# Turning one pass's x and results in 32x32 squares on VectorE instead of with TensorE transposes

## The chip, the cores and the metric

The kernel runs on one core of a Trainium2 chip. The metric is the device time of one execution in microseconds (us); less is better. Five engines matter. TensorE (PE in the profile; PEld is its weight load) multiplies matrices and writes the result to PSUM banks. VectorE (DVE), ScalarE (ACT) and GpSimd (POOL) work element by element. SyncE (SP) issues the transfers between memory (HBM) and the on-chip SBUF. Each engine carries out its own instructions strictly in order, and waits for other engines through semaphores.

## The reference

A layer of nine experts (eight gated by a probability per image, one shared) is added to its input. x holds 8 images of 512 rows by 256 features; an expert has a hidden width of 1,024.

```
g = einsum('bsd,edf->ebsf', h, Wg)
u = einsum('bsd,edf->ebsf', h, Wu)
expert_outs = einsum('ebsf,efd->ebsd', silu(g) * u, Wd)
expert_output = einsum('be,ebsd->bsd', gating_probs, expert_outs)
shared = (silu(h @ Sg) * (h @ Su)) @ Sd
x + (1 - sg) * expert_output + sg * shared
```

All of it is float32. Nothing in a row s of an image depends on another row, so the rows may stand in any order while they are worked on, if the same order is undone at the end.

## The kernel before

**Passes and units.** The 8 images are worked on in two passes (`h` = 0 and 1) of four images. A pass goes over 9 experts and 2 halves of the hidden width, so there are 36 units in all; a unit takes 66.9 us in the steady part of the trace. A unit has the "up" part, `gate_up` (products with Wg and Wu), and the "down" part of the unit before it, `down` (products with Wd), woven together by hand.

**The tiling.** The products use an algebraic scheme for fewer multiplications: for each of four images (index `i`) and each of six pairs of images (`PAIRS`), sums and differences of x and of weights are multiplied. For a pair the kernel needs three forms of x: `v`, a scaled difference, and two sums `b`. x has to stand turned for this, features on partitions and the 512 rows s along the free axis, in two halves `k` of 128 features. In the first pass `turn_x` makes the turned x and the first unit makes the forms (lines 238 and 252) and stores them to a scratch area in HBM (`store_forms`). All later units of the pass load the forms from there (lines 242 and 259: `v` has three buffers, `b` two).

**The second pass's x.** During the first pass `prepare(1)` makes the second pass's forms ahead of time: load an image in rows, turn it with TensorE transposes against the identity into a PSUM bank (`turn`, line 145, four 128x128 transposes make one turn of 128 features by 512 rows), copy it to SBUF with ScalarE (line 194) or combine it with VectorE (line 196), store it to `xdram`, load it back pair by pair, make the forms with GpSimd (lines 213 to 219) and store them (line 224). It is a generator. The main loop takes one step of it at every fifth "down" step from the third unit on, so its TensorE and GpSimd instructions stand between those of the units.

**The first pass's results.** They add up in SBUF tiles, `accb` and `accB`, one for each image and half of the features, features on partitions. When the pass closes, `turn_back` brings them back into rows: a turn of four transposes into a bank, then one VectorE addition of x's rows (line 634), and a store to `out` (line 635). x's rows come from `load_back` (line 616). The eight blocks of the first pass are turned back inside the second pass's first unit, at the "down" steps in `BACK_AT`, in the order of `BACK`. The second pass's results are turned at the end by the `h + 1 == NH` branch of the same function.

**The order of the work.** TensorE's and GpSimd's instructions are in the order in which the program writes them (`manual_schedule`), ScalarE's as well in the first unit. The order on the other engines and queues is chosen by a planner from its own idea of durations. All loads and stores go through SyncE's one queue, and every transfer there also waits for the landing of the one issued eight before it. The two PSUM banks that the down part shares with the turns are handed out by `new_po`; `turned[n]` notes that a turn used the bank last.

**Buffers.** The pool `io`, four buffers of 2 KB per partition, holds the rows, the turned blocks and the forms of `prepare`, and the rows of `load_back`.

Of the kernel before, what the change touches and what calls it, by code (L numbers as in the profile page):

```python
# [16 lines left out]
def kernel(  # L17
# [68 lines left out]
    dpool = ctx.enter_context(tc.tile_pool(name="d", bufs=2))  # L86
    iopool = ctx.enter_context(tc.tile_pool(name="io", bufs=4))
    dram = ctx.enter_context(
# [58 lines left out]
    def load_rows(pool, tag, b):  # L147
        rows = []
        for c in range(2):
            t = pool.tile([P, 2, D], F32, tag=tag, name=f"xin{b}_{c}")  # L150
            nc.sync.dma_start(
                t, x[b].rearrange("(p t) d -> p t d", t=NT)[:, 2 * c : 2 * c + 2, :]
            )
            rows.append(t)
        return rows

    def turn_x(h, rows):

        for i in range(NI):
            xt = xpool.tile([P, 2, S], F32, tag="x", name=f"x{h}_{i}")  # L160
            for n_, k in enumerate((0, 1) if CI[i] == 0.0 else (1, 0)):
                pt, n = new_po(f"ptx{h}_{i}_{k}")
                turn(pt, [rows[i][t // 2][:, t % 2, ts(k, P)] for t in range(NT)])
                turned[n] = True
# [12 lines left out]
    def prepare(h):  # L177

        def tile_of(name):
            return iopool.tile([P, S], F32, tag="io", name=f"{name}{h}")  # L180

        for i in range(NI):
            to = xdram[h, i] = dram.tile([P, 2, S], F32, tag=f"xd{h}_{i}", name=f"xd{h}_{i}")
            rows = load_rows(iopool, "io", NI * h + i)
            yield
            yield
            both = {}
            for k in (1, 0):
                pt, n = new_po(f"ptx{h}_{i}_{k}", True)
                turned[n] = True  # L190
                turn(pt, [rows[t // 2][:, t % 2, ts(k, P)] for t in range(NT)])
                both[k] = tile_of(f"xt{i}_{k}_")
                if k == 1 or CI[i] == 0.0:
                    nc.scalar.copy(both[k], pt)
                else:
                    ve.scalar_tensor_tensor(both[0], both[1], -CI[i], pt, ALU.mult, ALU.add)  # L196
                yield
            yield
            for k in (1, 0):
                nc.sync.dma_start(to[:, k], both[k])  # L200
            yield
        for p, (i, j) in enumerate(PAIRS):
            d = CI[i] - CI[j]
            to = dram.tile([P, 3, S], F32, tag=f"xs{h}_{p}", name=f"xs{h}_{p}")
            at = []
            for n, k in ((i, 0), (j, 0), (j, 1), (i, 1)):
                t = tile_of(f"f{p}_{n}_{k}_")
                nc.sync.dma_start(t, xdram[h, n][:, k])
                at.append(t)
            yield  # L210
            yield
            v = at[0]
            gp.tensor_tensor(v, v, at[1], ALU.subtract)
            if d != 1.0:
                gp.tensor_scalar(v, v, 1.0 / d, 0.0, ALU.mult, ALU.add)
            yield
            gp.tensor_tensor(at[2], v, at[2], ALU.add)
            yield
            gp.tensor_tensor(at[3], v, at[3], ALU.add)
            yield  # L220
            yield
            yield
            for k, n in ((0, 0), (1, 2), (2, 3)):
                nc.sync.dma_start(to[:, k], at[n])
            scratch[h, p] = to
            yield
# [380 lines left out]

    BACK = [(0, 1), (0, 0), (1, 1), (2, 1), (1, 0), (2, 0), (3, 1), (3, 0)]

    def block_of(a, b, r):  # L610
        return a[b].rearrange("(p t) d -> p t d", t=NT)[:, :, ts(r, P)]

    def load_back(h, i, r, pool=None, tag="io"):
        if (h, i, r) not in back:
            xr = (pool or iopool).tile([P, NT, P], F32, tag=tag, name=f"xr{h}_{i}_{r}")
            nc.sync.dma_start(xr, block_of(x, NI * h + i, r))
            back[h, i, r] = xr
        return back[h, i, r]

    def turn_back(h, i, r):  # L620

        b = NI * h + i
        block = ends.pop((h, i, r))
        pt, n = new_po(f"pto{b}_{r}", h + 1 < NH)
        turned[n] = True
        turn(pt, [block[:, ts(t, P)] for t in range(NT)])
        pt = pt.rearrange("p (t d) -> p t d", t=NT)
        if h + 1 == NH:
            for c, xr in enumerate(last_rows[i]):
                part = xr[:, :, ts(r, P)]  # L630
                ve.tensor_add(part, pt[:, 2 * c : 2 * c + 2], part)
            return
        xr = load_back(h, i, r)
        ve.tensor_add(xr, pt, xr)
        nc.sync.dma_start(block_of(out, b, r), xr)
        n = BACK.index((i, r)) + 1
        if n < len(BACK):
            load_back(h, *BACK[n])

# [128 lines left out]
    since_close = 1000  # L768
    BACK_AT = (5, 7, 9, 11, 14, 17, 20, 23)
    HAND = {mybir.EngineType.PE, mybir.EngineType.Pool}  # L770
# [20 lines left out]
    for u in units:  # L791
# [6 lines left out]
        for what in FIRST if u.n == 0 else LAST if nxt is None else ORDER:  # L798
            if what == "G":
# [6 lines left out]
                if final and nxt is not None and nG in (18, 21, 24, 27):  # L806
                    load_x(u.h + 1, (nG - 18) // 3)
                if nxt is None and nG == 40:
                    for i in range(NI):
# [77 lines left out]
```

## Time and profile before

| What | Value |
|---|---|
| time, median of 3 runs | 2461.21 us (2460.86 to 2461.64) |
| the profiled execution | 2461.27 us, span 2459.3 us |
| granted TensorE clock | 0.999 |
| loads (all `xin`, both passes, 256 KB each) | 24 |
| rows loaded by `load_back` (`xr`, 256 KB each) | 8, 3.1 us from issue to landing |
| results stored from `xr` (256 KB each) | 8, 3.5 us from issue to landing |
| `v`, `b` loaded from the scratch area | 210 each, 2.6 and 3.6 us |

One execution is profiled. The page gives for every engine its busy time and share of the span, and splits the span into 40 slices. A group of instructions has one line: source line, engine, operation, what it writes and reads, count, busy time, mean duration of one in ns, and the idle time of its engine just before it with the engine that ended it. The chain of waits is followed back from the last instruction, at each step to what released it. A busy time of TensorE includes the overlap of a matmul with the next, so two records that start 0.43 us apart show 0.59 us each. A float32 product shows as two records.

### The profile page before, as it was taken

To read this page: it belongs to the slowest core of one execution; us is meant where nothing else is said; L and a number is where in the kernel's file an instruction comes from. 1 tells how busy PE (TensorE), PEld (TensorE's weight loads), DVE (VectorE), ACT (ScalarE), POOL (GpSimd) and SP (SyncE) were. 2 spreads that over 40 slices of the span, in tenths; PEclk is the share of its full clock that TensorE was granted. 3 is DMA by queue.
4 is the path that set the end of the run, shared out by engine and by line. 5 is a ranking of instruction groups with operands and counts; after the bars stand their busy time and mean duration, and the time that the engine had idled before them with its cause. 6 is when DMAs were issued, how large, how long until landed. Compare 5 with 4: busy or idle time off the path is not lost.

```text
span 2459.3 us, 22816 instructions
## 1 busy us (share of the span) xinstructions
PE 2440.4 (99%) x5782; PEld 1084.0 (44%) x5782; DVE 1931.9 (79%) x2876; ACT 1246.4 (51%) x2305; POOL 2092.8 (85%) x2335
## 2 busy tenths in 40 slices
PE   9999999999999999999999999999999999999998
PEld 4444444444444444444444444444444444444444
DVE  7777787787777777777987777778777777777787
ACT  4555445545555555455455555555555555555543
POOL 7988888898898998888878888888888888888883
PEclk9999999999999999999999999999999999999999
DMA  5333333443333333333443233223333333223332
GB/s 168 95 93 103 97 113 107 124 132 107 109 115 94 119 97 106 110 116 113 127 144 94 88 90 98 86 86 99 99 103 103 94 103 90 86 89 96 91 93 82
DMA packets 180801, 255.83 MB, mean 104 GB/s; under 512 B 14016, under 2 KB 114368, under 8 KB 180672
## 3 DMA queue, kind: packets, MB, share of 16 engines
q1 hardware_dynamic: 180384, 254.33, 34.1%
q8 instruction: 49, 0.80, 0.1%
q14 instruction: 80, 0.66, 0.1%
q10 hardware_dynamic: 288, 0.04, 0.0%
HBM read 238.59 MB, written 15.73 MB: 103 GB/s over the span
## 4 chain that ended last, share of the span: by engine, by line
PE 89%; POOL 6%; DVE 2%; issue 1%; ACT 0%; DMA 0%; DVEq 0%; POOLq 0%; ACTq 0%
PE c L461 28%; PE c L451 14%; PE c L429 9%; PE c L407 9%; PE r L547 7%; PE r L570 7%; PE S L531 5%; PE b L531 5%; PE q L547 5%; PE s L547 2%; POOL cols L488 2%; POOL rows L488 1%; POOL wb L345 0%; DVE h L398 0%; POOL wb L346 0%
## 5 line engine op out<-in xcount | busy, mean ns | idle before, releaser
L461 PE MATMUL c<-b,wb 128*128 128x512 f32 x1728 | 847.3, 592 | 0.0
L393 ACT ACTIVATE sg<-c 128x512 f32<-128x512 f32 x576 | 343.6, 597 | 590.0 <-DVE c L466 336.9
L398 DVE SCALAR_TENSOR_TENSOR h<-sg,coef,c 128x512 f32<-128x512 f32 x576 | 428.1, 743 | 247.5 <-PE c L461 139.8
L461 PEld LDWEIGHTS c<-b,wb 128*128 128x128 f32 x1728 | 327.8, 190 | 410.0 <-issue 388.7
L451 PE MATMUL c<-v,u 128*128 128x512 f32 x864 | 441.7, 593 | 0.4 <-ACT c L446 0.3
L488 POOL TENSOR_TENSOR rows<-rows,h 128x512 f32<-128x512 f32 x282 | 371.1, 1316 | 0.0
L456 DVE TENSOR_TENSOR c<-D,c 128x512 f32<-128x512 f32 x432 | 299.1, 693 | 78.5 <-ACT sg L393 58.5
L488 POOL TENSOR_TENSOR cols<-cols,h 128x512 f32<-128x512 f32 x282 | 359.9, 1276 | 0.0
L466 DVE TENSOR_TENSOR c<-c,D 128x512 f32<-128x512 f32 x432 | 298.8, 692 | 20.1 <-PE c L461 19.9
L345 POOL TENSOR_TENSOR wb<-u,wb 128x256 f32<-128x256 f32 x108 | 79.0, 732 | 237.3 <-ACT wb L343 237.3
L407 PE MATMUL c<-x,w 128*128 128x512 f32 x576 | 277.9, 595 | 0.3 <-DVE x L168 0.3
L451 PEld LDWEIGHTS c<-v,u 128*128 128x128 f32 x864 | 162.9, 190 | 205.9 <-issue 165.3
L547 PE MATMUL r<-h,wd 128*128 128x512 f32 x426 | 217.7, 592 | 0.2 <-DVE xt L196 0.2
L570 PE MATMUL r<-X,ud 128*128 128x512 f32 x426 | 217.6, 592 | 0.0
L477 DVE TENSOR_TENSOR X<-h,h 128x512 f32<-128x512 f32 x213 | 210.4, 988 | 6.9
L429 PE MATMUL c<-x,at 128*128 128x512 f32 x432 | 209.6, 593 | 2.5 <-DVE P L422 2.2
L439 ACT COPY D<-c 128x512 f32<-128x512 f32 x284 | 165.9, 584 | 87.2 <-DVE h L398 87.2
L488 POOL TENSOR_TENSOR rows<-h,h 128x512 f32<-128x512 f32 x144 | 198.4, 1378 | 0.0
L488 POOL TENSOR_TENSOR cols<-h,h 128x512 f32<-128x512 f32 x144 | 184.2, 1279 | 0.0
L412 ACT COPY P<-c 128x512 f32<-128x512 f32 x216 | 126.6, 586 | 111.4 <-PE c L407 107.0
L407 PEld LDWEIGHTS c<-x,w 128*128 128x128 f32 x576 | 109.1, 191 | 135.0 <-issue 112.1
L530 ACT COPY S<-accS 128x512 f32<-128x512 f32 x134 | 79.1, 590 | 150.4 <-DVE accV L518 142.6
(105 smaller groups left out, 3482.4 us busy)
## 6 DMA issues: line engine op xcount, KB each, us to landing
b<-xs SPq DMA_DIRECT2D x210, 512.0 KB, 3.6
v<-xs SPq DMA_DIRECT2D x210, 256.0 KB, 2.6
w<-in_L_cond_Wg_dram SPq DMA_DIRECT2D x128, 128.0 KB, 3.5
w<-in_L_cond_Wu_dram SPq DMA_DIRECT2D x128, 128.0 KB, 3.6
wd<-in_L_cond_Wd_dram SPq DMA_DIRECT2D x32, 512.0 KB, 4.9
xin<-in_x_dram SPq DMA_DIRECT2D x24, 256.0 KB, 3.4
f<-xd SPq DMA_DIRECT2D x24, 256.0 KB, 3.2
xs<-f SPq DMA_DIRECT2D x18, 256.0 KB, 2.0
```

The costliest lines, as they stand in the source:

```text
L393: nc.scalar.activation(s, bank, AF.Silu)
L398: ve.scalar_tensor_tensor(t, u.sg[i, j], coef[:, u.e, b : b + 1], bank, ALU.mult, ALU.mult)
L407: nc.tensor.matmul(bank, u.raw[i][:, m, 0], xhub[u.h, i][:, 0], start=True, stop=True)
L429: nc.tensor.matmul(bank, u.at[i][:, m], xhub[u.h, i][:, 1], start=False, stop=True, skip_group_check=True,)
L451: nc.tensor.matmul(bank, u.U[p][:, m], u.V[p], start=False, stop=True, skip_group_check=True)
L456: ve.tensor_sub(other, u.Ds[j, m], bank)
L461: nc.tensor.matmul(bank, u.W[p][:, r, m], u.VB[p][:, r], start=False, stop=True, skip_group_check=True,)
L466: ve.tensor_add(bank, bank, u.Ds[j, m])
L488: gp.tensor_tensor(sums[n], u.h_[n, n] if first else sums[n], u.h_[at], ALU.add)
L531: nc.tensor.matmul(po, w, b, start=not full, stop=True, skip_group_check=full)
L547: nc.tensor.matmul(po, w, b, start=True, stop=True)
L570: nc.tensor.matmul(A, u.Ud[p], u.X[p], start=False, stop=True, skip_group_check=True)
```

## The change

The second pass's x and the first pass's results are no longer turned by TensorE. VectorE's `transpose` takes a 128x512 tile as a grid of 32x32 squares and turns each square by itself, leaving the square where it is. The squares are brought to their places by the transfers:

- `load_turned` loads an image for `prepare` with eight DMAs in place of two. Each takes 32 features of the image to 32 partitions, in runs of 32 elements (128 bytes). Two VectorE transposes and one subtraction (none for image 0) give the turned x. The copies on ScalarE fall away.
- The first pass's rows s stand in another order along the free axis, such that a square of a result block holds 32 features of rows 16 apart: `turn_x` writes its transposes into the bank with a stride.
- `turn_back` transposes a result block in squares into a tile of the pool `z`, and adds it to x's rows, which `load_back` has loaded in squares (four DMAs per image, runs of 128 bytes). Both halves of an image share a tile, and are stored with four DMAs, in runs of 128 bytes. The end of the second pass is turned as before.
- `BACK`, `BACK_AT` and the places of the first loads differ: images 0 and 2 are loaded in the last unit of the first pass, image 1 takes the tile of image 0 after its store, image 3 that of image 2.
- The pool `io` has two buffers of 4 KB in place of four of 2 KB, and the forms of `prepare` load both halves of an image at once.

```diff
--- before.py
+++ after.py
@@ -84,7 +84,7 @@
     zpool = ctx.enter_context(tc.tile_pool(name="z", bufs=6))
     spool = ctx.enter_context(tc.tile_pool(name="s", bufs=4))
     dpool = ctx.enter_context(tc.tile_pool(name="d", bufs=2))
-    iopool = ctx.enter_context(tc.tile_pool(name="io", bufs=4))
+    iopool = ctx.enter_context(tc.tile_pool(name="io", bufs=2))
     dram = ctx.enter_context(
         tc.tile_pool(name="dram", bufs=1, space=bass.MemoryType.DRAM)
     )
@@ -147,20 +147,43 @@
     def load_rows(pool, tag, b):
         rows = []
         for c in range(2):
-            t = pool.tile([P, 2, D], F32, tag=tag, name=f"xin{b}_{c}")
+            if pool is not iopool:
+                t = pool.tile([P, 2, D], F32, tag=tag, name=f"xin{b}_{c}")
+            elif c == 0:
+                both = pool.tile([P, NT, D], F32, tag=tag, name=f"xin{b}")
+            if pool is iopool:
+                t = both[:, 2 * c : 2 * c + 2]
             nc.sync.dma_start(
                 t, x[b].rearrange("(p t) d -> p t d", t=NT)[:, 2 * c : 2 * c + 2, :]
             )
             rows.append(t)
         return rows
 
+
+    def squares(a, b, q):
+
+        return a[b].rearrange("s (k q d) -> q s k d", k=2, d=32)[q]
+
+    def load_turned(to, b):
+
+
+        at = x[b].rearrange("(c r t) d -> r t c d", r=32, t=NT)
+        for k in (1, 0):
+            for q in range(4):
+                nc.sync.dma_start(
+                    to[ts(q, 32), k].rearrange("r (t c d) -> r t c d", t=NT, d=32),
+                    at[:, :, :, ts(4 * k + q, 32)],
+                )
+
     def turn_x(h, rows):
 
         for i in range(NI):
             xt = xpool.tile([P, 2, S], F32, tag="x", name=f"x{h}_{i}")
             for n_, k in enumerate((0, 1) if CI[i] == 0.0 else (1, 0)):
                 pt, n = new_po(f"ptx{h}_{i}_{k}")
-                turn(pt, [rows[i][t // 2][:, t % 2, ts(k, P)] for t in range(NT)])
+                at = pt.rearrange("d (l t h) -> d t h l", l=4, h=32)
+                for t in range(NT):
+                    nc.tensor.transpose(at[:, t], rows[i][t // 2][:, t % 2, ts(k, P)], ident)
                 turned[n] = True
                 if k == 1:
                     nc.scalar.copy(xt[:, 1], pt)
@@ -177,51 +200,48 @@
     def prepare(h):
 
         def tile_of(name):
-            return iopool.tile([P, S], F32, tag="io", name=f"{name}{h}")
+            return iopool.tile([P, 2, S], F32, tag="io", name=f"{name}{h}")
 
         for i in range(NI):
             to = xdram[h, i] = dram.tile([P, 2, S], F32, tag=f"xd{h}_{i}", name=f"xd{h}_{i}")
-            rows = load_rows(iopool, "io", NI * h + i)
-            yield
-            yield
-            both = {}
+            rows = tile_of(f"xin{i}_")
+            load_turned(rows, NI * h + i)
+            yield
+            yield
+            both = tile_of(f"xt{i}_")
             for k in (1, 0):
-                pt, n = new_po(f"ptx{h}_{i}_{k}", True)
-                turned[n] = True
-                turn(pt, [rows[t // 2][:, t % 2, ts(k, P)] for t in range(NT)])
-                both[k] = tile_of(f"xt{i}_{k}_")
-                if k == 1 or CI[i] == 0.0:
-                    nc.scalar.copy(both[k], pt)
-                else:
-                    ve.scalar_tensor_tensor(both[0], both[1], -CI[i], pt, ALU.mult, ALU.add)
+                ve.transpose(both[:, k], rows[:, k])
+                if k == 0 and CI[i] != 0.0:
+                    ve.scalar_tensor_tensor(
+                        both[:, 0], both[:, 1], -CI[i], both[:, 0], ALU.mult, ALU.add
+                    )
                 yield
             yield
             for k in (1, 0):
-                nc.sync.dma_start(to[:, k], both[k])
+                nc.sync.dma_start(to[:, k], both[:, k])
             yield
         for p, (i, j) in enumerate(PAIRS):
             d = CI[i] - CI[j]
             to = dram.tile([P, 3, S], F32, tag=f"xs{h}_{p}", name=f"xs{h}_{p}")
-            at = []
-            for n, k in ((i, 0), (j, 0), (j, 1), (i, 1)):
-                t = tile_of(f"f{p}_{n}_{k}_")
-                nc.sync.dma_start(t, xdram[h, n][:, k])
-                at.append(t)
-            yield
-            yield
-            v = at[0]
-            gp.tensor_tensor(v, v, at[1], ALU.subtract)
+            at = {}
+            for n in (i, j):
+                at[n] = tile_of(f"f{p}_{n}_")
+                nc.sync.dma_start(at[n], xdram[h, n])
+            yield
+            yield
+            v, B_i, B_j = at[i][:, 0], at[i][:, 1], at[j][:, 1]
+            gp.tensor_tensor(v, v, at[j][:, 0], ALU.subtract)
             if d != 1.0:
                 gp.tensor_scalar(v, v, 1.0 / d, 0.0, ALU.mult, ALU.add)
             yield
-            gp.tensor_tensor(at[2], v, at[2], ALU.add)
-            yield
-            gp.tensor_tensor(at[3], v, at[3], ALU.add)
-            yield
-            yield
-            yield
-            for k, n in ((0, 0), (1, 2), (2, 3)):
-                nc.sync.dma_start(to[:, k], at[n])
+            gp.tensor_tensor(B_j, v, B_j, ALU.add)
+            yield
+            gp.tensor_tensor(B_i, v, B_i, ALU.add)
+            yield
+            yield
+            yield
+            for k, made in enumerate((v, B_j, B_i)):
+                nc.sync.dma_start(to[:, k], made)
             scratch[h, p] = to
             yield
 
@@ -605,37 +625,39 @@
                     ends[u.h, i, r] = acc["bB"[r], i]
             yield
 
-    BACK = [(0, 1), (0, 0), (1, 1), (2, 1), (1, 0), (2, 0), (3, 1), (3, 0)]
-
-    def block_of(a, b, r):
-        return a[b].rearrange("(p t) d -> p t d", t=NT)[:, :, ts(r, P)]
-
-    def load_back(h, i, r, pool=None, tag="io"):
-        if (h, i, r) not in back:
-            xr = (pool or iopool).tile([P, NT, P], F32, tag=tag, name=f"xr{h}_{i}_{r}")
-            nc.sync.dma_start(xr, block_of(x, NI * h + i, r))
-            back[h, i, r] = xr
-        return back[h, i, r]
+    BACK = [(0, 1), (0, 0), (2, 1), (2, 0), (1, 1), (1, 0), (3, 1), (3, 0)]
+
+    def load_back(h, i):
+
+        if (h, i) not in back:
+            xr = iopool.tile([P, S // 32, 2, 32], F32, tag="io", name=f"xr{h}_{i}")
+            for q in range(4):
+                nc.sync.dma_start(xr[ts(q, 32)], squares(x, NI * h + i, q))
+            back[h, i] = xr
+        return back[h, i]
 
     def turn_back(h, i, r):
 
         b = NI * h + i
         block = ends.pop((h, i, r))
-        pt, n = new_po(f"pto{b}_{r}", h + 1 < NH)
-        turned[n] = True
-        turn(pt, [block[:, ts(t, P)] for t in range(NT)])
-        pt = pt.rearrange("p (t d) -> p t d", t=NT)
         if h + 1 == NH:
+            pt, n = new_po(f"pto{b}_{r}")
+            turned[n] = True
+            turn(pt, [block[:, ts(t, P)] for t in range(NT)])
+            pt = pt.rearrange("p (t d) -> p t d", t=NT)
             for c, xr in enumerate(last_rows[i]):
                 part = xr[:, :, ts(r, P)]
                 ve.tensor_add(part, pt[:, 2 * c : 2 * c + 2], part)
             return
-        xr = load_back(h, i, r)
-        ve.tensor_add(xr, pt, xr)
-        nc.sync.dma_start(block_of(out, b, r), xr)
-        n = BACK.index((i, r)) + 1
-        if n < len(BACK):
-            load_back(h, *BACK[n])
+        xr = load_back(h, i)
+        t = zpool.tile([P, S], F32, tag="z", name=f"to{b}_{r}")
+        ve.transpose(t, block)
+        ve.tensor_add(xr[:, :, r], t.rearrange("p (c d) -> p c d", d=32), xr[:, :, r])
+        if (i, 1 - r) not in BACK[BACK.index((i, r)):]:
+            for q in range(4):
+                nc.sync.dma_start(squares(out, b, q), xr[ts(q, 32)])
+            if i in (0, 2):
+                load_back(h, i + 1)
 
     last_rows = {}
     tails = {}
@@ -766,7 +788,7 @@
 
     ends = {}
     since_close = 1000
-    BACK_AT = (5, 7, 9, 11, 14, 17, 20, 23)
+    BACK_AT = (5,10,11,13,15,18,20,23)
     HAND = {mybir.EngineType.PE, mybir.EngineType.Pool}
     by_hand = ExitStack()
     by_hand.enter_context(
@@ -805,6 +827,8 @@
                     behind = down(u, acc)
                 if final and nxt is not None and nG in (18, 21, 24, 27):
                     load_x(u.h + 1, (nG - 18) // 3)
+                if final and nxt is not None and nG in (30, 36):
+                    load_back(u.h, (nG - 30) // 3)
                 if nxt is None and nG == 40:
                     for i in range(NI):
                         last_rows[i] = load_rows(
```

## The prediction

> **What bounds the kernel now.** I read the page first, its engine row and its chain of waits; then the groups by form; then the chain around the change of passes, the busy time by stretches, and the DMA queues in short windows. From the page:
>
> ```profile
> PE 2440.4 (99%) x5782; PEld 1084.0 (44%) x5782; DVE 1931.9 (79%) x2876; ACT 1246.4 (51%) x2305; POOL 2092.8 (85%) x2335
> ```
>
> TensorE is busy for 99% of the span, and in the steady units the chain is TensorE alone. A product counts as two records of 0.43 us there, so what leaves TensorE shortens the run by its own length, unless another engine is the late one at that place. Two places are such: the first 100 us and some 15 us after the change of passes. The sum is made against the profiled execution, 2461.27 us; its span is 2459.3 us, and the median of the runs shown is 2461.21 us, 0.06 us lower, so no correction is needed.
>
> The groups by form (the first within 150 to 450 us; count, then busy us and mean ns, then idle time before and who ended it):
>
> ```profile
> L145 PE MATMUL ptx<-ident,xin 128*128 128x128 f32 x32 | 4.9, 276 | 1.8 <-ACT accS L539 1.8
> ...
> L477 DVE TENSOR_TENSOR X<-h,h 128x512 f32<-128x512 f32 x213 | 210.4, 988 | 6.9
> ...
> L168 DVE COPY x<-ptx 128x512 f32<-128x512 f32 x1 | 0.7, 691 | 5.7 <-PE ptx L145 5.7
> ```
>
> The chain after the change of passes (start, us, what):
>
> ```profile
> 1239.83 0.68 DVE xr L634
> 1240.51 1.20 DVE accb L522 x2
> 1241.71 1.41 DVE P L422 x3
> 1243.12 0.29 issue
> 1243.41 1.88 DVE P L422 x3
> 1245.29 0.61 DVE accB L518
> 1245.90 0.04 issue
> 1245.95 0.66 PE pto L145 x4
> 1246.60 0.86 PE c L451 x2
> ...
> 1257.34 0.44 PE pto L145 x4
> ```
>
> Here VectorE is the late engine from 1239.8 to 1245.9 us. From 1246 us on TensorE is again, and a turn of four transposes costs 0.44 us of chain.
>
> Busy time by stretches (us: length, then PE, PEld, DVE, ACT, POOL with their counts, clock, DMA share, GB/s):
>
> ```profile
> 12.00:48.00 36.00, 34.13 (x90) 14.55 (x88) 35.15 (x49) 19.21 (x39) 31.93 (x39) 1.00 0.46 160
> 48.00:66.00 18.00, 18.00 (x42) 7.50 (x42) 15.01 (x19) 9.10 (x19) 18.00 (x18) 1.00 0.41 136
> 1250.00:1283.00 33.00, 33.00 (x94) 15.54 (x93) 24.74 (x36) 17.49 (x33) 20.69 (x22) 1.00 0.64 192
> ```
>
> VectorE is full in the first stretch (35.15 of 36 us) and has room in the other two.
>
> **Part 1, the second pass's x.** Eight turns leave TensorE's order: 8 x 0.44 = 3.5 us. With them goes the 1.8 us in which TensorE stood ahead of them, waiting until ScalarE had emptied the shared bank (first group row). Behind them the ordinary products follow, whose inputs are ready; nothing else is late there. Gain 5.3 us. Five ScalarE copies of 0.59 us go too, hidden now and then.
>
> In their place come eight turns on VectorE and the three subtractions that were there before. Their order isn't written by hand, and in the changed program's order they have all moved to the first two units: two transposes stand between the forms of v at about 31 and 36 us, three instructions between 48 and 66 us, six between 78 and 103 us. No 32x32 turn is in this trace. The nearest row is the 128x512 float32 copy, 0.69 us. The Trainium skill, page "VectorE: DVE Perf Modes", section "The three transpose paths", gives 311 ns for 128x128 in bf16; four of those make 1.24 us, an estimate. It speaks against the change: 0.55 us more for each of 16 turns. I take the row, which has this size and type; 1.24 us is the upper end, and the 0.34 us of the fastest VectorE instruction on 128x512 here (v, L240 at 41.69 us: 0.41 us, with its overlap removed) the lower.
>
> The first two stand in a full stretch: 2 x 0.69 = +1.4 us, between 0.7 and 2.5. The next three are 2.1 us in a stretch with 3.0 us of VectorE idle. But TensorE takes nothing there that is ready long before, so between nothing and 2.1 us; I take the middle, +1.0. The last six fall where VectorE has 8.5 us idle of 32 (66 to 98 us) and more after: nothing, at most 1 us if they stand ahead of a wanted subtraction.
>
> SyncE's order gains 32 loads of 512 runs for eight of 128. A load of 512 runs held its queue for 0.55 us (xr, L616), so 17.6 us in place of about 3, all from 12 to 103 us, past the stores of v and b, the weights and the first v and b of unit 1. The queue stands idle for more than half of that time. The nearest need behind it is the third weight tile of unit 1, issued at 56.8 us, landing 3.6 us later and used by GpSimd at 67.7: 7 us of cover against four loads, 2.2 us. Two transposes, at about 51 and 62 us, may wait for their last load up to 1 us; that is in the bounds above. Stores of the turned x wait for VectorE with other transfers queued behind, but the turns stand well ahead of those transfers' own waits. Nothing more taken.
>
> The first pass's 32 transposes now write their bank in strides of 32 and 4 places. No strided write to a bank is in this trace: between nothing and a doubling of 8 x 0.44 us. I take nothing, for loads of x hold this stage.
>
> **Part 2, the pass's results.** Eight turns leave TensorE. The first two stand in the VectorE-bound stretch: there the first turn and addition on VectorE (0.69 + 0.99 for 0.68 us) make the chain 1.0 us longer, which eats the two turns of 0.44 and most of the 0.6 us of waiting for accB at 1245.3. I count these as zero. The six others give 6 x 0.44 = 2.6 us.
>
> VectorE pays. An addition no longer reads a bank but two operands beside GpSimd's work, like X: 0.99 us in place of 0.69. By the changed order, seven turns and seven additions fall between 1250 and 1283 us, where five additions stood: 24.74 - 5 x 0.69 + 7 x 0.69 + 7 x 0.99 = 33.1 us, in a stretch that TensorE would now do in 33 - 5 x 0.44 = 30.8 us. **VectorE becomes the bound there** by 2.3 us: loss 2.3, from nothing (additions at 0.69, the rest fitted around) to 5.
>
> **The transfers of part 2.** Rows of 512 bytes become squares of 128: per image 4,096 packets, 256 on each of 16 DMA engines. Two windows, 0 to 9 us and 1290 to 1294 us, give the price of a packet (packets, MB, share):
>
> ```profile
> q10 hardware_dynamic: 288, 0.04, 2.3%
> ```
> ```profile
> q1 hardware_dynamic: 672, 0.79, 64.6%
> ```
>
> The first is the gates, packets of 256 bytes and fewer: 2.3% of 16 x 9 us is 3.3 us, 11.5 ns a packet. The second is one store of 512-byte rows and 128 packets of 4 KB: 41.3 us, of which the large ones at 19 GB/s take 27.6, so about 27 ns per 512-byte row. For 128 bytes I take 11.5 ns, an image 2.9 us. The rule against it is in the Trainium skill, page "DMA: Bandwidth & Descriptors", "Specifications": under 512 bytes the DMA reads, modifies and writes. Nothing in this trace shows a short store. By the rule a store might cost two 512-byte accesses, 54 ns, 13.8 us an image.
>
> SyncE's queue: by four points (0.32 us at 128 runs, 0.55 at 512) 1,024 runs hold it about 0.86 us, an image 3.5 us. The order is: four stores of image 0 (ready about 1254 us), the b of the third pair, four loads of image 1, which wait for those stores, four stores of image 2, then the b of the fourth pair. That b went out here:
>
> ```profile
> 1265.64 0.38 SPq L259 DMA_DIRECT2D b<-xs  x1
> ```
>
> Its product starts at 1275.0 us, some 1274 without the turns. Now it lands at 1254 + 3.5 + 2 (stores landed) + 3.5 + 3.5 + 3.5 + up to 1 = about 1271: cover 3 us, no cost. With packets over 13.7 ns the packets rule in place of the issues: 1259.5 + 0.768 us per ns, which reaches 1274 at **19 ns**. Beyond that TensorE waits.
>
> **Sum:** 2461.27 - 5.3 + 1.4 + 1.0 - 2.6 + 2.3 = 2458.1; I say 2458.0 us.
>
> **Rivals.**
> A, **short packets (slower):** place, b of the fourth pair; from 19 ns. At 27 ns it lands at 1280.2: +6.2, 2464 us. With stores at 54 and loads at 27 it lands at 1294: +20, 2478 us; with loads at 11.5, +16, 2474. For it: the rule, and a DMA share of 0.64 already in that stretch. Against: the gates' packets, which are loads.
> B, **VectorE hides it:** startup and overload fit into idle time, only the turns count: 2461.27 - 5.3 - 3.5 = 2452.5 us. For it: VectorE's 79%; against: the full first stretch.
> C, **slow turn** (1.24 us): +0.55 for two turns at the start, about 1 for the next, 8 x 0.55 at the change of passes: +6.5, 2464.5 us. For it the skill's figure, against it the rows[...], all 0.69.
>
> **How the numbers follow.** Forecast 0.38, A 0.30, C 0.14, B 0.18. A measurement of this kernel tells about 0.2% (4.9 us) from no change: bounds 2456.3 and 2466.1. Faster: B and 0.12 of the forecast, 0.30. Slower: 0.26 of A (which may add to C) and 0.08 of C, 0.34. Within: 0.36. The range goes from B to A's stores at 54 ns with loads at 11.5: 2452 to 2474; the forecast's own is 2454 to 2462.
>
> **What would show it.** Right: no TensorE wait ahead of a turn at 180 to 430 us; TensorE some 2 us later at 100 us; VectorE near full from 1250 to 1283; the turn at 0.6 to 0.7 us; 128-byte packets near 12 ns, and no wait of b's products for a DMA. Wrong: b's products waiting for xs at 1265 to 1290, VectorE waiting for loads of x, or a turn over 1 us.

## The result, and the profile after

| | Kernel before | Kernel after |
|---|---|---|
| time, median | 2460.91 us (2460.62 to 2461.64) | 2454.39 us (2453.63 to 2455.2) |
| the profiled execution's span | 2459.3 us | 2452.9 us |
| granted TensorE clock | 0.999 | 0.999 |

The ratio is 0.9974, with a 95% interval of 0.9965 to 0.9983: the changed kernel is 6.5 us faster, between 4.2 and 8.6. That is 3.6 us below the forecast of 2458.0, at the lower end of its own range (2454 to 2462), and by 1.6 us past the 4.9 us that the forecast took for the limit of "no change"; it had given 0.30 to such a gain.

From the page of the kernel after, the engine row:

```profile
PE 2432.8 (99%) x5718; PEld 1077.7 (44%) x5718; DVE 1940.2 (79%) x2890; ACT 1245.8 (51%) x2304; POOL 2094.4 (85%) x2335
```

TensorE has 64 records less: sixteen turns of four. Its busy time fell by 7.6 us, VectorE's rose by 8.3.

Busy time by stretches, kernel after, the three stretches that the forecast used:

```profile
12.00:48.00 36.00, 33.36 (x90) 14.63 (x88) 34.48 (x50) 18.71 (x37) 30.58 (x38) 1.00 0.57 180
48.00:66.00 18.00, 16.94 (x40) 6.80 (x39) 15.50 (x20) 8.14 (x18) 16.64 (x16) 1.00 0.54 165
...
1250.00:1283.00 33.00, 33.00 (x78) 14.63 (x77) 30.53 (x45) 16.26 (x32) 22.84 (x23) 1.00 0.81 176
```

At the start TensorE lost 0.8 us in the first stretch and 1.1 in the second (34.13 and 18.00 before). At the change of passes it has no gap at all, and VectorE is busy for 30.5 us, not for the 33.1 that the forecast had worked out, though 45 instructions are in it, as many as were counted (36 before, less five, plus fourteen).

The new operations, by tile (shortest/median/longest in ns, first and last start):

```profile
L213 DVE STREAM_TRANSPOSE xt<-xin x8: 697/700/711, 32.7 to 107.5; 128x512 f32<-128x512 f32 x8
```
```profile
L655 DVE TENSOR_TENSOR xr<-to,xr x8: 677/733/1751, 1238.0 to 1280.2; 128x512 f32<-128x512 f32 x8
```

A turn of 128x512 in squares takes 0.70 us (0.69 forecast). The additions, taken at 0.99 us each, have a median of 0.73.

Where TensorE waits in the first 136 us, by its timeline. The bracket at the end of a line is the idle time before it and who ended it. Kernel after:

```profile
21.10 2.23 PE L449 MATMUL c<-x,at 128*128 128x512 f32 x4 [0.24 <-POOL wb L366]
27.42 1.12 PE L449 MATMUL c<-x,at 128*128 128x512 f32 x2 [1.51 <-DVE P L442]
35.91 1.13 PE L471 MATMUL c<-v,u 128*128 128x512 f32 x2 [0.43 <-ACT c L466]
40.06 1.13 PE L471 MATMUL c<-v,u 128*128 128x512 f32 x2 [0.45 <-ACT c L466]
56.88 1.13 PE L471 MATMUL c<-v,u 128*128 128x512 f32 x2 [1.06 <-ACT c L466]
94.06 1.13 PE L449 MATMUL c<-x,at 128*128 128x512 f32 x2 [0.45 <-DVE P L442]
98.31 1.12 PE L567 MATMUL q<-cols,ad 128*128 128x512 f32 x2 [0.55 <-POOL cols L508]
```

The waits add up to 4.69 us; the same view of the kernel before has four, of 0.36, 1.09, 0.33 and 0.60, 2.38 in all. Between 130 and 430 us the kernel after has no wait in this view.

Such a sum is that of one execution. Four of the experiments below (e4, e9, e10, e14) run the same program up to the change of passes, and the sums of their profiled executions are 4.15, 3.68, 5.22 and 5.06 us. They begin differently: from 9 to 11 us the granted clock was 0.50 in the execution shown and 1.00 in that of e10, whose products then stand 1.6 us earlier at 21 us and lose a part of it again in waits. So a difference of 1 us between two such sums tells little, and the medians decide.

At the change of passes, TensorE's timeline, first before, then after:

```profile
1243.55 1.13 PE L429 MATMUL c<-x,at 128*128 128x512 f32 x2 [0.49 <-DVE P L422]
1245.95 0.66 PE L145 MATMUL pto<-ident,accb 128*128 128x128 f32 x4 [0.41 <-DVE accB L518]
```
```profile
1240.64 1.13 PE L449 MATMUL c<-x,at 128*128 128x512 f32 x2 [1.64 <-DVE P L442]
```

Two waits of 0.9 us became one of 1.64: the first turn and its addition stand ahead of the subtractions P on VectorE (its timeline, kernel after):

```profile
1236.21 0.70 DVE L654 STREAM_TRANSPOSE to<-accB 128x512 f32<-128x512 f32 x1
1236.83 1.25 DVE L542 SCALAR_TENSOR_TENSOR accb<-r,accb 128x512 f32<-128x512 f32 x2
1238.01 0.79 DVE L655 TENSOR_TENSOR xr<-to,xr 128x512 f32<-128x512 f32 x1
1238.72 3.66 DVE L442 TENSOR_TENSOR P<-P,c 128x512 f32<-128x512 f32 x6
```

The short packets: a DMA window of the kernel after in which only four stores of squares run (1247 to 1251.5 us), its queue row with packets, MB and share of 16 engines:

```profile
q1 hardware_dynamic: 3327, 0.42, 54.7%
```

54.7% of 16 x 4.5 us over 3,327 packets is 11.8 ns a packet (11.5 forecast). So much for stores: the read-modify-write that the Trainium skill states for transfers under 512 bytes ("DMA: Bandwidth & Descriptors", "Specifications") leaves no mark in the time of a packet here; the 54 ns that rival A estimated from it are more than four times what was measured.

### The profile page after: what moved, and what is told of

The parts are those of the page before. It is cut to its first block, busy times and chain, and to the rows that moved or that the text cites. A ratio compares the mean times of both kernels' runs of the same rounds, so it can differ in the third digit from the quotient of the medians.

```text
span 2452.9 us, 22735 instructions
## 1 busy us (share of the span) xinstructions
PE 2432.8 (99%) x5718; PEld 1077.7 (44%) x5718; DVE 1940.2 (79%) x2890; ACT 1245.8 (51%) x2304; POOL 2094.4 (85%) x2335
## 4 chain that ended last, share of the span: by engine, by line
PE 90%; POOL 6%; DVE 2%; issue 1%; DMA 0%; ACT 0%; SPq 0%; DVEq 0%; POOLq 0%; ACTq 0%
PE c L481 28%; PE c L471 14%; PE c L449 9%; PE c L427 9%; PE r L567 7%; PE r L590 7%; PE S L551 5%; PE b L551 5%; PE q L567 5%; PE s L567 2%; POOL cols L508 1%; POOL rows L508 1%; POOL wb L365 0%; DVE h L418 0%; POOL u L353 0%
## 5 line engine op out<-in xcount | busy, mean ns | idle before, releaser
L508 POOL TENSOR_TENSOR cols<-h,h 128x512 f32<-128x512 f32 x144 | 184.7, 1282 | 0.0
```

What stands on the lines that cost most here:

```text
L508: gp.tensor_tensor(sums[n], u.h_[n, n] if first else sums[n], u.h_[at], ALU.add)
```

## The experiments

All times are medians in us; the kernel before ran beside each group of runs, at 2460.6 to 2460.9 us. Unless a diff says otherwise it is against the kernel after.

| Run | Time | Against after |
|---|---|---|
| e1_part1_alone | 2456.74 | +2.4 |
| e2_part2_alone | 2458.01 | +3.6 |
| e3_turns_held | 2471.57 | +17.2 |
| e4_first_add_later | 2458.4 | +4.0 |
| e7_no_early_transposes | 2451.98 | -2.4 |
| e8_hold_two_turns_earlier | 2472.11 | +17.7 |
| e9_four_more_transposes | 2457.58 | +3.2 |
| e10_eight_more_transposes | 2459.77 | +5.4 |
| e11_turns_behind_unit_2 | 2452.17 | -2.2 |
| e12_turns_behind_unit_1 | 2452.06 | -2.3 |
| e14_square_loads_twice | 2459.14 | +4.8 |

### Each part alone

The first run keeps the new `prepare` and turns the results as before; the second keeps the new results (with the strided `turn_x`) and prepares x as before. Their cores:

```diff
# e1_part1_alone, turn_back
-        t = zpool.tile([P, S], F32, tag="z", name=f"to{b}_{r}")
-        ve.transpose(t, block)
+        pt, n = new_po(f"pto{b}_{r}", h + 1 < NH)
+        turn(pt, [block[:, ts(t, P)] for t in range(NT)])
...
+        ve.tensor_add(xr, pt, xr)
+        nc.sync.dma_start(block_of(out, b, r), xr)
# e2_part2_alone, prepare
-            load_turned(rows, NI * h + i)
+            rows = load_rows(iopool, "io", NI * h + i)
...
-                ve.transpose(both[:, k], rows[:, k])
+                turn(pt, [rows[t // 2][:, t % 2, ts(k, P)] for t in range(NT)])
```

> Part 1 alone: the second pass's x turned in squares on VectorE, the first pass's results turned by TensorE as before and the first pass's x with its rows in the old order. Theory: the eight turns (3.5 us) and TensorE's waits ahead of and behind them at 190 to 340 us (2.4 us) go, the start up to 136 us loses 2.4 us to the early VectorE turns: 3.5 us faster than before, 2457.4. Rival (the start's loss comes from the first pass's strided bank writes, which are not in here): no loss at the start, 6 us faster, 2455.

> Part 2 alone: results turned back in squares on VectorE, first pass's transposes with strided writes, the second pass's x turned by TensorE and ScalarE as before. Theory: the turns go (3.5 us), the wait after the change of passes is 0.4 us longer than before, the start stays as it was: 3.1 us faster, 2457.8. Rival (the strided writes are the start's loss): 2.4 us of waits more before 136 us, 0.7 us faster, 2460.2.

Measured against before: -3.9 us (ratio 0.9985, 0.9976 to 0.9994) and -2.6 us (0.999, 0.9981 to 0.9998). The parts add up to the whole, -6.5. The forecast had -2.9 for the first and -0.3 for the second: it misjudged the second part by 2.3 us and the first by 1.0. Both theories hold within 0.7 us, and both rivals fall by 1.7 us or more. The first run's waits up to 136 us are 3.73 us, though, 1.35 more than before and not the 2.4 of its theory. The strided writes of the first pass's turns cost nothing that can be told: the second run has them and no early VectorE turns, and its waits up to 136 us (3.54 us) lie 1.2 above the kernel before, but kernels with the same strided writes and no early turns (e7, e11, e12 below) show 2.6 to 2.8; and the first run, without the strided writes, waits as long as e9, which has them (3.73 and 3.68).

### The change of passes: has VectorE time in hand?

```diff
# e9_four_more_transposes (e10_eight_more_transposes: range(2))
         ve.transpose(t, block)
+        if i in (2, 1):
+            ve.transpose(t, block)
```

> The kernel after with the four transposes of images 2 and 1 at the change of passes (1249 to 1260 us) made twice, the second over the first: 4 x 0.70 = 2.8 us more on VectorE in its full stretch. Step of the forecast (33 us of work for 31 us of span, what is over is paid in whole): 2457.2 us, 2.8 us above the kernel after. Theory (VectorE lags behind there without TensorE noticing, since TensorE's order runs ahead of it, and its gaps from 1265 us take the lag up): at most 1 us, 2454.4 to 2455.4.

> As the run with four more, but each of the four transposes made three times: 5.6 us more on VectorE. Step of the forecast: 2460.0 us, 5.6 above the kernel after. Theory: the lag outgrows what the order has in hand, and something of it is paid: 2456 to 2458, clearly less than 5.6 us more.

My theory fell. 2.8 us more of VectorE cost 3.2 us, 5.6 us more cost 5.4: all of it is paid, within what these runs can tell. SyncE's transfers stand in the same order as in the kernel after. Busy time from 1250 to 1264 us, kernel after:

```profile
1250.00:1264.00 14.00, 14.00 (x34) 6.16 (x33) 13.95 (x22) 8.64 (x17) 8.66 (x9) 1.00 0.88 175
```

TensorE 14.00 and VectorE 13.95 of 14 us: both are full, and neither waits for the other. One more instruction on VectorE and TensorE does wait, as the timeline of the run with four more shows:

```profile
1260.49 1.10 PE L471 MATMUL c<-v,u 128*128 128x512 f32 x2 [0.46 <-issue]
1265.27 1.13 PE L471 MATMUL c<-v,u 128*128 128x512 f32 x2 [1.11 <-ACT c L466]
1270.77 1.10 PE L471 MATMUL c<-v,u 128*128 128x512 f32 x2 [0.94 <-POOL wb L366]
1314.67 1.12 PE L567 MATMUL q<-cols,ad 128*128 128x512 f32 x2 [0.75 <-POOL cols L508]
```

The last line lies 50 us behind the added work. The chain of waits of this run goes back from there over GpSimd's sums to a load of Wu, to SyncE, to the landing of a store of squares and to the addition before it: a late addition holds the store, the store holds the tile and SyncE's queue, and the next unit's weights come late. Of the 3.3 us of waits shown, 1.7 end with GpSimd (wb and cols): half of the price is paid there, in a place that the forecast did not have.

So the forecast's step "what VectorE has over is paid in whole" holds in its size; the amount over was wrong. The forecast's stretch starts in the kernel after at 1246 us, as that is 4.0 us ahead there by the same products, and takes TensorE 30.8 us:

```profile
1246.00:1276.80 30.80, 30.80 (x74) 13.58 (x73) 28.32 (x44) 17.55 (x34) 20.19 (x23) 1.00 0.79 165
```

VectorE is busy for 28.3 us of it, not for 33.1: full up to 1265 us, with gaps behind. Line by line, the stretch has the same 31 other instructions as in the kernel before (and 0.03 us of one more), and all seven turns. The sum was too high by 4.8 us for three reasons. Of the seven additions only five are in it; they take 4.2 us where seven at 0.99 would be 6.9, and the last two, 2.35 us together, start at 1278.56, where VectorE has room again: 2.7 us. The three sums X<-h,h take 0.93 us each in place of 1.22: 0.9 us. The other 1.1 us or so is a fault of the sum: it added whole records to a busy time, and in a full queue a record begins before the one ahead of it has ended (VectorE's timeline, kernel after):

```profile
1258.22 0.70 DVE L654 STREAM_TRANSPOSE to<-accB 128x512 f32<-128x512 f32 x1
1258.84 0.66 DVE L654 STREAM_TRANSPOSE to<-accb 128x512 f32<-128x512 f32 x1
1259.44 0.70 DVE L418 SCALAR_TENSOR_TENSOR h<-sg,coef,c 128x512 f32<-128x512 f32 x1
```

From start to start these are 0.62 and 0.60 us.

### The first addition later

```diff
-    BACK_AT = (5,10,11,13,15,18,20,23)
+    BACK_AT = (9,10,11,13,15,18,20,23)
```

> The changed kernel with the first block of results turned back four down steps later (9 in place of 5). Its transpose may still stand early in VectorE's order, its addition comes behind the six subtractions of the hub. Theory: the 1.8 us wait of TensorE at 1238 us holds that addition's own place, 0.7 us or more: 0.7 us faster than the changed kernel, 2453.7, wait down to about 1.1. Rival (the wait only moves to the next late instruction, since VectorE is full up to 1250 us): same as the changed kernel within 0.2 us.

The wait at 1240 us fell from 1.64 to 0.93, as expected, and yet the run lost 4.0 us. The planner had put SyncE's instructions in another order: a store of image 2, which could not start before 1259.17 us, went ahead of the loads of image 1, and these, the other stores and then the next b stood behind it. TensorE's timeline of this run:

```profile
1269.60 1.10 PE L481 MATMUL c<-b,wb 128*128 128x512 f32 x2 [1.25 <-DMA b<-xs]
1314.06 1.39 PE L567 MATMUL q<-cols,ad 128*128 128x512 f32 x2 [1.94 <-POOL cols L508]
```

b went out at 1265.49 us; in the kernel after it went out here (SyncE's timeline):

```profile
1253.08 4.01 SPq L635 DMA_DIRECT2D xr<-in_x_dram  x4
1258.32 2.78 SPq L658 DMA_DIRECT2D out_dram<-xr  x4
1261.20 0.63 SPq L279 DMA_DIRECT2D b<-xs  x1
```

Neither the theory nor the rival had this loss. The run doesn't tell what the first addition's place is worth, since two things differ.

### More short packets

```diff
-            for q in range(4):
-                nc.sync.dma_start(xr[ts(q, 32)], squares(x, NI * h + i, q))
+            for _ in range(2 if i in (1, 3) else 1):
+                for q in range(4):
+                    nc.sync.dma_start(xr[ts(q, 32)], squares(x, NI * h + i, q))
```

> The kernel after with the four loads of x's squares of images 1 and 3 at the change of passes issued twice, the second over the first: per image 4,096 more packets of 128 bytes and some 4 us more of SyncE's queue, ahead of the b of the fourth and of the fifth pair. VectorE's work is the same. Step of the forecast (b has 3 us in hand, the transfers cost nothing until that is used up): 1 to 2 us of wait of TensorE for that b and as much again for the fifth, 2456 to 2458. Rival A of the forecast (transfers rule here): each 4 us is paid, and what is late behind b (the weights of the next unit, GpSimd's forms) as well: 2462 or more. If there is far more in hand than the forecast said, 2454 to 2455.

Between the two: 4.8 us more than the kernel after. The b of the fourth pair went out 2.2 us later and nothing waited for it. The b of the fifth went out at 1273.37 in place of 1267.70 us, 5.7 later, and was waited for:

```profile
1278.84 2.05 PE L481 MATMUL c<-b,wb 128*128 128x512 f32 x2 [2.78 <-DMA b<-xs]
```

So that b had 3 to 4 us in hand: 5.7 less 2.78, and TensorE stood 0.9 us earlier in this execution. The forecast had 3 us, but for the pair before. Behind the wait the same product takes 2.05 us in place of 1.1, and there is again a later wait for GpSimd, 0.8 us at 1316. Rival A's price of a packet was wrong, but a b, though that of the next pair, was not far from late: 4 us more on the queue per image were enough.

### The start: VectorE or transfers?

```diff
-            both = tile_of(f"xt{i}_")
+            both = rows
             for k in (1, 0):
-                ve.transpose(both[:, k], rows[:, k])
-                if k == 0 and CI[i] != 0.0:
-                    ve.scalar_tensor_tensor(
-                        both[:, 0], both[:, 1], -CI[i], both[:, 0], ALU.mult, ALU.add
-                    )
                 yield
```

> The kernel after, but the preparation stores the loaded squares as they are: its eight VectorE transposes and its subtractions are left out, so the second pass computes with other x; all loads and stores stay where they were. Theory (the 2.5 us more that TensorE waits before 136 us are VectorE's time: five transposes of 0.70 us and the subtractions stand in VectorE's full queue of that stretch): TensorE's waits before 136 us fall back to what the kernel before shows, and the time to 2451.4 us, 3 us below the kernel after. Rival (the loss is the transfers: 128-byte runs on SyncE's queue and on the DMA engines delay the weights of the first group): the waits stay and the time is 2454 to 2455.

2451.98 us, 2.4 below the kernel after; TensorE's waits up to 136 us are 2.63 us (4.69 after, 2.38 before), though all 32 loads of squares run there. So the loss hangs on the turns in VectorE's order, and the rival as it was written falls: the loads by themselves hold nothing up. But leaving out a turn leaves out its wait for its load too, and the transfers have a part there. In the kernel after the third turn finds its load late, the sum b behind it takes long, and TensorE waits 1.06 us at 57 us; in the profiled execution of e9, the same program up to there, the load is in time and TensorE has no wait at that place. VectorE's timeline, kernel after, then e9:

```profile
51.98 0.71 DVE L213 STREAM_TRANSPOSE xt<-xin 128x512 f32<-128x512 f32 x1 [0.52 <-DMA xin<-in_x_dram]
53.79 1.76 DVE L272 TENSOR_TENSOR b<-v,x 128x512 f32<-128x512 f32 x1
```
```profile
51.42 0.71 DVE L213 STREAM_TRANSPOSE xt<-xin 128x512 f32<-128x512 f32 x1
53.23 1.11 DVE L272 TENSOR_TENSOR b<-v,x 128x512 f32<-128x512 f32 x1
```

The executions of e4, e10 and e14 have the late load, the long b and the wait, as the kernel after has. What makes b long is not shown.

### Holding the turns: two ways that fail

```diff
# e3_turns_held
+            gp.memset(rows[:, :, 0:1], 0.0)
             load_turned(rows, NI * h + i)
# e8_hold_two_turns_earlier
+            gp.memset(rows[:, :, 0:1], 0.0)
+            yield
+            yield
             load_turned(rows, NI * h + i)
```

> The changed kernel with the loads for the second pass's x held at the place in the order where they are written, by one GpSimd memset of a column of each tile that the loads then overwrite; so the VectorE turns fall into steady units from the third on. Theory: the start's loss is the early place of the turns, and steady units have room on VectorE: 2.4 us faster than the changed kernel, 2452.0, and waits before 136 us back to some 9 us. Rival (VectorE at 79% has no room in a steady unit either, or late turns hold up SyncE's queue): TensorE waits 0.5 us or more at each of the four images, and the gain is under 1 us or none.

> The kernel after, with a GpSimd memset on the target of each turned load, two steps of the preparation ahead of the load (in the earlier experiment it stood right ahead of it). GpSimd's order is written by hand, so the load and the transposes can't go ahead of the third group. Theory (the earlier experiment lost 17 us only since the load left GpSimd's late instruction when VectorE's transpose was already next in its queue): with some 30 us between the memset and the place of the load, the data is there, no transpose makes VectorE wait, the start's waits fall to those of the kernel before, and the time is 2451.4 us. Rival (any tie of the loads to GpSimd is late, as the planner believes GpSimd to be ahead of where it is): VectorE again waits some us at a transpose, and the time is above 2458.

In both the start was repaired (TensorE waits 2.57 and 3.01 us up to 136 us) and 17 us were lost against the kernel after. Each run has two long waits of TensorE instead: they end at 168.78 us (9.60 us long) and 254.33 (4.77) in the first, at 168.28 (9.64) and 386.23 (6.98) in the second. For the first run neither the theory nor the rival had waits of this size. Timelines of GpSimd and TensorE in the second, and of VectorE in the first:

```profile
160.37 0.10 POOL L208 MEMSET xin<- 128x2 f32 x1
```
```profile
157.62 1.02 PE L474 MATMUL c<-v,u 128*128 128x512 f32 x2
168.28 2.08 PE L452 MATMUL c<-x,at 128*128 128x512 f32 x2 [9.64 <-DVE P L445]
```
```profile
166.24 0.71 DVE L214 STREAM_TRANSPOSE xt<-xin 128x512 f32<-128x512 f32 x1 [9.77 <-DMA xin<-in_x_dram]
166.88 1.25 DVE L443 TENSOR_TENSOR P<-P,c 128x512 f32<-128x512 f32 x2
```

GpSimd works without a gap and reaches the memset at 160.4 us. Only then do the loads leave SyncE. VectorE had been at the turn since some 156 us (166.24 less 9.77 in the first run) and stood there, with the subtractions P behind it for which TensorE waits. VectorE's order, the planner's, thus has the turn ahead of subtractions that were ready; that the planner believed GpSimd to be there earlier is inferred from this order. Moving the load by two steps changed nothing, because the memset stood where it had stood. The theory written for e8 fell, the rival held.

### A hold that works

```diff
# e11_turns_behind_unit_2 (e12_turns_behind_unit_1: units[0])
             both = tile_of(f"xt{i}_")
+            if i == 0:
+                late = units[1].h_[3, 2][:, 0:2]
+                ve.tensor_copy(both[:, :, 0:1], late.rearrange("p (k o) -> p k o", o=1))
```

> The kernel after, with one VectorE copy of 128x2 elements from the last h tile of the second unit (made at about 148 us) into the target of the first two transposes. The loads stay early; the eight transposes and three subtractions of the preparation now stand behind 148 us in VectorE's order. Theory (the start's loss is VectorE's time there, as the run without the transposes showed with 2.4 us; the two GpSimd holds failed by the lag of GpSimd behind the plan, which this tie doesn't use): TensorE's waits before 136 us as in the kernel before, no transpose waits for a load or for GpSimd, time 2451.4 to 2452, 2.4 to 3 us below the kernel after. Rival (any later place costs as much, because the planner's order then lets SyncE's stores and loads of the preparation stand in front of the weights of units 2 and 3): a wait of over 2 us at 150 to 260 us, time 2454 or more.

> The same with the last h tile of the first unit (about 103 us): the transposes stand behind 100 us, where VectorE has idle time of 1 to 2 us before every second h. Theory: as the other, 2451.4 to 2452; if the waits at 93 to 100 us of the kernel after (0.6 and 0.7 us) come from the transposes, they go too. Rival as for the other.

2452.17 us (2451.31 to 2452.3) and 2452.06 us (2451.76 to 2453.08), against 2453.63 to 2455.2 for the kernel after: 2.2 and 2.3 us less, about what leaving the turns out gave. The intervals of the ratios to before overlap with that of the kernel after, but the times themselves don't. The tie is to a result of VectorE itself, so nothing can be late for it that VectorE didn't make late; the loads stay early. TensorE's timeline of e12 up to 136 us:

```profile
20.68 2.23 PE L452 MATMUL c<-x,at 128*128 128x512 f32 x4 [0.17 <-DVE f L447]
26.58 1.12 PE L452 MATMUL c<-x,at 128*128 128x512 f32 x2 [1.10 <-DVE P L445]
46.68 1.12 PE L474 MATMUL c<-v,u 128*128 128x512 f32 x2 [0.72 <-ACT c L469]
95.72 1.13 PE L570 MATMUL q<-cols,ad 128*128 128x512 f32 x2 [0.76 <-POOL cols L511]
```

2.75 us in all. The two waits near 36 and 40 us and the one at 57 us of the kernel after have become one of 0.72. With a ratio of 0.9965 to before (0.9952 to 0.9977), it and e11 (0.9964), which can't be told apart, are the fastest of the versions that do the whole work.

## Why the prediction was right or wrong

- **Sixteen turns.** The forecast took 14 x 0.44 us off the path and counted the first two of the results as eaten. Right: with the wait at 1240 us 0.74 us longer, those two left 0.14. (The working was loose: its own 1.0 us against 0.88 for the turns and 0.6 of waiting would have left a gain of 0.5.)
- **TensorE's waits ahead of `prepare`'s turns.** Forecast 1.8 us. From 180 to 350 us TensorE was busy for 168.03 of 170 us before and is for 170.00 after: 1.97.
- **The start.** Forecast +1.4 for the first two turns, +1.0 for the next three, nothing for the last six. The sum held: the waits grew by 2.31 us in the profiled execution, and by the medians the three runs without early turns gave back 2.2 to 2.4. The parts did not, so that the sum came out with luck. Of the first stretch's 0.85 us more, 0.30 stand at 21 and 27 us, ahead of the first turn at 32.7; 0.55 are left for the first two turns. The next three have 1.06 us at 57 us, in those executions in which a load is late; the forecast had this wait for a load within its bounds. The last six are not free: at 94 and 98 us there are 0.40 us more, and the wait for P at 94 us (0.45) is in every profiled execution with early turns and in none without.
- **VectorE's overload at the change of passes, +2.3 us: the step that failed.** That VectorE is full there and that more is paid is right, as the added turns show; the size is not. TensorE lost nothing: VectorE's work in the stretch is 28.3 us, less than TensorE's 30.8, since two additions lie behind it (2.7 us with the shorter ones), the sums X are shorter (0.9) and records of a full queue overlap (1.1). The bound "nothing (additions at 0.69, the rest fitted around)" was the value, and it is 2.3 of the 3.6 us by which the forecast was off. The second point (0.2), the first (0.1) and the start (0.1) make 0.4 more. Another 0.36 is the starting value: the sum began at 2461.27 us, and the median of the kernel before is 2460.91 in the result. The last 0.5 us lie within the interval and were not traced.
- **Short packets at no cost.** Right in the price (11.8 ns) and in the cover, though it was the fifth pair's b, not the fourth's, that stood nearest to its need.
- **The turn's price.** The copy's row gave 0.69, measured 0.70; the estimate of 1.24 from the Trainium skill's 128x128 bf16 figure ("VectorE: DVE Perf Modes", "The three transpose paths") is refuted for this size and type. Rival C falls.
- **The rivals.** B, "VectorE hides it all", gave 2452.5 us, and the result, 2454.39, is nearer to it than to the forecast's 2458.0. At the change of passes it came true in the time, but with nothing to spare up to 1265 us; at the start it was wrong.

## What to carry to other kernels

Where a sum says that an engine gets just over full, the outcome can hang on where a planner puts the last two instructions: give that term both bounds, and test the place by doubling the added work. For a full queue, add the distances from start to start, not the lengths of the records. Work that an engine must do "sometime early" is best tied to a late result of that same engine; here a tie to another, backlogged engine turned its lag into a wait of the whole queue behind it. And when instructions are moved on one engine, look at what the planner then does with the queue of the transfers.

## What the runs showed of the hardware that was not expected

A long wait of TensorE costs more than its length. Granted clock behind the 9.64 us wait of e8 (windows, clock in the third column from the end):

```profile
168.00:172.00 4.00, 3.72 (x5) 1.66 (x6) 3.23 (x6) 1.07 (x2) 0.00 (x0) 0.50 0.02 6
172.00:180.00 8.00, 8.00 (x20) 3.46 (x19) 4.15 (x6) 5.43 (x10) 0.73 (x1) 0.96 0.21 66
```

For about 4 us products took twice their time, some 2 us more. The same stood behind the 2.78 us wait of e14 (clock 0.52 from 1278.8 to 1282 us), and not behind the 2.27 us wait of e10 (1.00 from 1266 to 1269 us). The Trainium skill ("TensorE: Matmul & The Clock Gate", "HAM oscillation — how this bites in real kernels") warns of idle gaps over about 3.4 us; from the start of the last record ahead of it to the next product, the gap of e14 is 3.4 us long and that of e10 2.9. Where between the two the limit lies is not shown. A forecast of a wait near 3 us has to allow for this.

The additions of two SBUF operands on VectorE (xr, L655) took from 0.68 to 1.75 us for the same shape, and SyncE gave 0.70 us to a store of 1,024 runs but 1.0 us to a load of as many (2.78 and 4.01 us for four).
